# Rows through DRAM in place of PE's fan-out, constants in the order of need, and a new table of turns

## The chip, the cores and the metric

The kernel runs on one core of a Trainium2 chip. The metric is the device time of one execution in microseconds (us); the lower the better. All data are float32, except the adjacency matrix, which is int32.

## The reference

A batch of 32 graphs, each with 512 nodes of 256 features (`x`) and a 512 x 512 adjacency matrix (`adj`), goes through two layers. Both layers are a graph attention and a feed-forward part, each on the layer norm of `x` and added to `x`.

```
x += gat0(norm(x), adj)          # attention over neighbours, W and a
x += mamba2(norm(x))             # in-projection, causal conv of 4, scan over the
                                 # sequence in 8 heads of 64, 64 states, gate, out
x += gru(gat1(norm(x), adj), norm(x))
x += shared_mlp(norm(x)) + experts(norm(x))   # 4 experts, the best 2 weighted
```

Attention: `softmax(mask(leaky_relu(f1_i + f2_j, 0.2)))`, where f1 and f2 are products of a node's features with a vector. Since exp of a leaky relu is the larger of two products of a factor of the query and a factor of the key, the kernel needs two rows of 512 query factors on all 128 partitions. Mamba's scan needs, for chunks of 128 steps, the decay of the carried states for each head and step: exp of a cumulative sum, again a row on 64 partitions. The experts need the gate of each node on the 64 partitions that hold an expert's hidden units.

## The kernel before

The 32 elements of the batch are worked on one after the other and interleaved: each element passes through 20 parts (`PARTS`): `load_x`, `load_adj`, `gnn0`, `mamba`, `steps_of_time`, two convolutions, `products_of_bc`, `gate_of_z`, `scan`, `output`, `load_adj`, `gnn1`, two halves of the GRU, `gru_out`, `moe`, `gates`, `experts`, `mixture`. Every part is a generator that yields after each step, most steps being one instruction of one engine or a group of matmuls. `PLAN` gives each step a turn, and element b's steps come `PERIOD` turns after those of element b - 1. The steps of all elements, sorted by turn, are the program; each engine works through its share of it in that order and waits by semaphores for what it needs. In `PLAN` every turn modulo `PERIOD` is used once (420 steps, period 420), so a turn is a rank and not a time; one element's steps stretch over five periods.

Tiles rotate: `bank` (8 PSUM banks of 512 floats a partition), `big` (4), `quad` (16), `row` (26 of 512 floats). `x` and the adjacency rows are loaded, and the result stored, by DMAs that SP issues, in the same program order.

Three places put rows on many partitions with PE:

- `attention` (in both layers): `f1` of each 128 nodes is broadcast along the free dimension and transposed against `ident` (L290, four 128x128 transposes into `pf`), so that all partitions hold the 512 values. ACT makes the two factors of 128x512 from it (L294 relu, L297 exp, two each). `top`, `nf` and `nfs` (L276 to L285) are the maximum of the keys and its multiples. Then ACT and DVE build `pT` (L309 to L315), the weights of attention, for ps_h (layer 0, L343) or ps_g (layer 1, L675).
- `steps_of_time`: `byL` holds cumulative sums, 32 rows for each chunk c. After the ps_seg matmuls (L445) 24 matmul records with `kind1` (L461) put them on 64 partitions per head, into three banks `ps_ecs`, and ACT's exp makes `ecs` of three of the chunks (L468). `scan` uses them (L577, L579, L620).
- `gates`: the five columns of gates and a one are written four times over (`g5`, L797 to L807), transposed by four transposes (`ps_gT`, L812) and copied (`gT`, L815). `mixture` multiplies them with `pair_of` (L868) to put each expert's gate on 64 partitions, and adds the biases by matmuls on two row groups (L873); DVE multiplies (L877), PE sums the experts (L884, L886) and DVE adds to `x` (L888).

Float32 matmuls show as two records each, transposes as one.

Ahead of the loop come the constants: ACT issues most of their DMAs, SP those of layer 0's attention. PE multiplies weights there (`wc` L159, `wih` L174, `wrow` L125), and a pool `once` holds what only these need.

Of the kernel before, what the change touches and what calls it, by code (L numbers as in the profile page):

```python
# [11 lines left out]
F32 = mybir.dt.float32  # L12
# [6 lines left out]
P = 128  # L19
# [12 lines left out]
def adj_ffn_kernel(ctx: ExitStack, tc: tile.TileContext, i: dict, out: bass.AP):  # L32
# [5 lines left out]
    psum = ctx.enter_context(tc.tile_pool(name="psum", bufs=8, space=bass.MemoryType.PSUM))  # L38

# [4 lines left out]
    def big(name):  # L44
        return bigs.tile([P, T, N], F32, tag="big", name=name, bufs=4)
# [10 lines left out]
    stage = ExitStack()  # L56
    once = stage.enter_context(tc.tile_pool(name="once", bufs=1))
# [11 lines left out]
    pair_of = const.tile([HD, P], F32, name="pair_of")  # L69
    for j in range(2):  # L70
        nc.vector.tensor_copy(pair_of[32 * j:32 * j + 32].rearrange("e (s g) -> e s g", s=2),
                              ident[32 * j:32 * j + 32, 34 * j:34 * j + 2].unsqueeze(2).to_broadcast([32, 2, HD]))
# [8 lines left out]
    kind1 = const.tile([P, HD], F32, name="kind1")  # L81
    nc.vector.tensor_copy(kind1, kinds[:, 1:].to_broadcast([P, HD]))
# [3 lines left out]
    def load(name, shape, src, pool=const):  # L86
        t_ = pool.tile(shape, F32, name=name)
        nc.scalar.dma_start(t_, src)
        return t_
# [4 lines left out]
    def gat_columns(l, w, queue):  # L94

        ab = once.tile([P, 2 * D], F32, name="ab", tag="ab")
        queue.dma_start(ab, i[f"L{l}_gnn_a"].partition_broadcast(P))
        prod = once.tile([P, D], F32, name="prod", tag="prod")
        cols = once.tile([P, 2, KD], F32, name="cols", tag="cols")
        for k in range(KD):  # L100
            for s in range(2):
                nc.vector.scalar_tensor_tensor(prod, w[:, k, :D], 1.0, ab[:, s * D:(s + 1) * D], op0=ALU.mult,
                                               op1=ALU.mult, accum_out=cols[:, 1 - s, k:k + 1])
        return cols


# [4 lines left out]
    w_last = once.tile([P, D], F32, name="w_last")  # L111
    nc.sync.dma_start(w_last, i["L0_gnn_W"][D - 1].partition_broadcast(P))
    for k in range(KD):
        nc.vector.tensor_sub(we[:, k, :D], we[:, k, :D], w_last)
    nc.gpsimd.memset(we[:, 0, D:], 0.0)
    nc.vector.tensor_copy(we[:, 1, D:], ident[:, P - 1:])

    def on_all(l, w, queue):

        cols = gat_columns(l, w, queue)  # L120
        row_ = const.tile([P, 2, D], F32, name=f"wrow{l}")
        ps = bank("ps_wrow")
        for u in range(2):
            for k in range(KD):
                nc.tensor.transpose(ps[:, u * D + k * P:u * D + (k + 1) * P],  # L125
                                    cols[:, u, k:k + 1].to_broadcast([P, P]), ident)
        nc.vector.tensor_copy(row_.rearrange("p u d -> p (u d)"), ps)
        return row_

    wrow0 = on_all(0, we, nc.sync)  # L130
    scales = const.tile([P, 3], F32, name="scales")
    for n, v in enumerate((0.2, 0.8, -0.8)):
        nc.gpsimd.memset(scales[:, n:n + 1], v)


    win = load("win", [P, KD, 1160], kchunks(i["L0_ffn_W_in"]))
    nc.gpsimd.tensor_scalar(win[:, :, :512], win[:, :, :512], 0.5, 1.0, op0=ALU.mult, op1=ALU.mult)
    wdt = const.tile([P, KD, 32], F32, name="wdt")
    nc.gpsimd.memset(wdt, 0.0)
    nc.vector.tensor_copy(wdt[:, :, :HEADS], win[:, :, 1152:])  # L140
    cw = load("cw", [P, 5, 4], i["conv_w"])
    nc.vector.tensor_scalar_mul(cw, cw, 0.5)
    cb = load("cb", [P, 5], i["conv_b"])
    nc.vector.tensor_scalar_mul(cb, cb, 0.5)
    dtb = load("dtb", [P, HEADS], i["L0_ffn_dt_bias"].partition_broadcast(P))
    posneg = const.tile([P, 2, HEADS], F32, name="posneg")
    nc.scalar.dma_start(posneg[:, 0, :], i["L0_ffn_A_log"].partition_broadcast(P))
    nc.scalar.activation(posneg[:, 0, :], posneg[:, 0, :], AF.Exp)
    nc.vector.tensor_scalar_mul(posneg[:, 1, :], posneg[:, 0, :], -1.0)
# [3 lines left out]
    woutT = load("woutT", [P, KD, 512], kchunks(i["woutT"]), once)  # L153
    wlin = load("wlin", [P, KD, D], kchunks(i["L0_ffn_W_lin"]), once)
    wc = const.tile([P, NP, D], F32, name="wc")
    for j in range(NP):
        ps = bank("ps_wc")
        for k in range(KD):
            nc.tensor.matmul(ps[:, :D], woutT[:, k, j * P:(j + 1) * P], wlin[:, k, :], start=k == 0,  # L159
                             stop=k == KD - 1)  # L160
        nc.vector.tensor_scalar_mul(wc[:, j, :], ps[:, :D], normw[:, j:j + 1])


    w = load("w", [P, KD, D], kchunks(i["L1_gnn_W"]), once)
    wrow1 = on_all(1, w, nc.scalar)
    wT = load("wT", [P, KD, D], kchunks(i["L1_gnn_WT"]), once)
    raw = load("raw", [P, KD, 3 * D], kchunks(i["wihT"]), once)
    wih = const.tile([P, KD, 3 * D], F32, name="wih")
    for m in range(KD):
        for cols in (slice(0, 2 * D), slice(2 * D, 3 * D)):  # L170
            ps = bank("ps_wih")
            n = cols.stop - cols.start
            for k in range(KD):
                nc.tensor.matmul(ps[:, :n], wT[:, k, m * P:(m + 1) * P], raw[:, k, cols], start=k == 0,  # L174
                                 stop=k == KD - 1)
            nc.vector.tensor_copy(wih[:, m, cols], ps[:, :n])
# [3 lines left out]
    brz = const.tile([P, 4], F32, name="brz")  # L180
    nc.vector.tensor_add(brz, bih[:, :4], bhh[:, :4])
    nc.vector.tensor_scalar_mul(brz, brz, 0.5)

# [6 lines left out]
    for e in range(4):  # L190
        nc.scalar.dma_start(ew1[:, :, e, :], kchunks(i["L1_ffn_eW1"][e]))
# [6 lines left out]
    for r in (64, 96):  # L198
        nc.scalar.dma_start(b3[r:r + 4, :], i["L1_ffn_eb3"])
        nc.scalar.dma_start(b3[r + 4:r + 5, :], i["L1_ffn_sb3"].unsqueeze(0))  # L200
    gw = const.tile([P, KD, 32], F32, name="gw")
    nc.gpsimd.memset(gw, 0.0)
    nc.scalar.dma_start(gw[:, :, :4], kchunks(i["L1_ffn_gW"]))
    gb = load("gb", [P, 4], i["L1_ffn_gb"].partition_broadcast(P))

# [5 lines left out]

    stage.close()
    bigs = ctx.enter_context(tc.tile_pool(name="bigs", bufs=1))
    work = ctx.enter_context(tc.tile_pool(name="work", bufs=1))
    small = ctx.enter_context(tc.tile_pool(name="small", bufs=2))
# [41 lines left out]
    def load_x(e):  # L257
        e.x = quad("x", T)
        nc.sync.dma_start(e.x, x_in[e.b].rearrange("(t p) d -> p t d", p=P))
        yield  # L260

    def load_adj(e):

        e.adj = []
        for j in range(T):
            a_ = row("adj", I32)
            nc.sync.dma_start(a_, adjT_in[e.b, j * P:(j + 1) * P, :])
            e.adj.append(a_)
            yield

    def attention(f1, f2, adj, kind):

        top = small.tile([P, 1], F32, name="top")
# [8 lines left out]
        nfs = small.tile([P, 3], F32, name="nfs")  # L284
        nc.vector.tensor_scalar_mul(nfs, scales, nf)  # L285
# [3 lines left out]
        for t in range(T):  # L289
            nc.tensor.transpose(pf[:, t * P:(t + 1) * P], f1[:, t:t + 1].to_broadcast([P, P]), ident)  # L290
        yield
        query = quad("query", 2)
        for n, scale in enumerate((-0.8, 0.8)):
            nc.scalar.activation(query[:, n, :], pf, AF.Relu, scale=scale, bias=nfs[:, n + 1:n + 2])  # L294
            yield
        for n in range(2):
            nc.scalar.activation(query[:, n, :], query[:, n, :], AF.Exp, scale=-1.0)  # L297
            yield
# [7 lines left out]
        for j in range(0, T, 2):  # L306
            both = [(i, pT[:, i, :]) for i in (j, j + 1)]
            for i, p in both:
                nc.scalar.activation(p, query[:, 0, :], AF.Identity, scale=key1[:, i:i + 1])  # L309
                yield  # L310
            for i, p in both:
                nc.vector.scalar_tensor_tensor(p, query[:, 1, :], key2[:, i:i + 1], p, op0=ALU.mult, op1=ALU.max)  # L312
                yield
            for i, p in both:
                nc.vector.scalar_tensor_tensor(p, adj[i].bitcast(kind), 2.0 ** -120, p, op0=ALU.max, op1=ALU.min)  # L315
                yield
        return pT

    def scores(xn, wrow):

        f21 = small.tile([P, 2, T], F32, name="f21")
        for u in range(2):
            for t in range(T):
# [3 lines left out]
                yield  # L327
        return f21

    def gnn0(e):  # L330
# [4 lines left out]
        f21 = yield from scores(xn, wrow0)  # L335

        pT = yield from attention(f21[:, 1, :], f21[:, 0, :], e.adj, U32)
# [28 lines left out]
    def narrow(name, w, vT):  # L366
# [8 lines left out]
        few = small.tile([P, P], F32, name="fewT")  # L375
# [6 lines left out]
    def steps_of_time(e):  # L382
# [51 lines left out]
        yield  # L434
        byHL = quad("byHL", HEADS)
# [5 lines left out]
        e.ecss = [None]  # L441
        for h0 in (0, 4):
# [5 lines left out]
            for c in range(0, T, 2):  # L448
# [4 lines left out]
                for L, _ in both:  # L453
                    nc.scalar.activation(L, L, AF.Exp, scale=-1.0)
                    yield

        banks = [bank("ps_ecs") for c in range(1, T)]
        for q in range(2):
            for c, ps in enumerate(banks, 1):
# [435 lines left out]
    class Element:  # L895
        def __init__(self, b):
            self.b = b
# [97 lines left out]
```

## Time and profile before

| | |
|---|---|
| median of 3 runs | 3431.39 us (3430.87 to 3433.0) |
| profiled execution: its own time | 3430.99 us |
| its span, from the first to the last instruction | 3429.3 us |
| granted clock of TensorE, mean | 0.996 |
| PE / DVE / ACT / POOL busy | 3367.4 / 2814.7 / 1694.0 / 587.8 us |
| DMA: packets, MB | 78392, 110.45 |
| first ps_h (L343) | at 38.0 us |
| landing of adj (256 KB) / x (512 KB) / the result (512 KB), median | 2.8 / 3.9 / 5.3 us |

PE is TensorE's matmuls, PEld its weight loads, DVE VectorE, ACT ScalarE, POOL GpSimd, SP SyncE. A busy time is the time during which at least one instruction of the engine runs; matmuls are pipelined and overlap, so what one costs is better read from the distance between the starts of neighbours. "Idle before" names what an engine waited for. L with a number is a line of the kernel above.

### The profile page before, as it was taken

The page shows a single profiled execution, that of the slowest core. Times are in us where ns is not written, and L with a number is a line of the kernel's source. Part 1 is how long each engine was busy: PE and PEld are TensorE (multiplying, and loading weights), DVE is VectorE, ACT ScalarE, POOL GpSimd, SP SyncE. Part 2 cuts the span into 40 slices and gives each one's busy share as a digit, 9 for nine tenths or more (in the row PEclk, how much of TensorE's full clock was granted, in tenths as well). Part 3 has the DMA queues.
Part 4 walks back from the last instruction along what each step waited for, and adds up shares of the span by engine and source line. Part 5 has one row for each costly group of instructions (what it writes and reads, how often), then busy time and mean ns, then how long its engine had stood idle before and what let it go on. Part 6 is the DMA issues. An engine that isn't in the chain of part 4 may idle for free.

```text
span 3429.3 us, 49262 instructions
## 1 busy us (share of the span) xinstructions
PE 3367.4 (98%) x17800; PEld 1979.2 (58%) x17800; DVE 2814.7 (82%) x7625; ACT 1694.0 (49%) x3202; POOL 587.8 (17%) x593
## 2 busy tenths in 40 slices
PE   5999999999999999999999999999999999999998
PEld 3555655565555656555655556565556555565654
DVE  6888888888888888888888888888888888888873
ACT  2455455444555454554445554445544455544453
POOL 0112111112111121111121111221111211112210
PEclk8999999999999999999999999999999999999999
DMA  3001011011001010110110110101101100101000
GB/s 127 22 28 38 22 38 28 25 38 38 23 28 34 29 38 22 37 28 25 38 38 22 28 34 29 38 22 38 28 26 38 38 22 28 35 28 38 19 19 13
DMA packets 78392, 110.45 MB, mean 32 GB/s; under 512 B 8122, under 2 KB 44100, under 8 KB 78148
## 3 DMA queue, kind: packets, MB, share of 16 engines
q1 hardware_dynamic: 71216, 101.34, 9.9%
q10 hardware_dynamic: 6932, 5.96, 0.5%
q8 instruction: 141, 2.31, 0.3%
q14 instruction: 103, 0.84, 0.1%
HBM read 90.50 MB, written 16.78 MB: 31 GB/s over the span
## 4 chain that ended last, share of the span: by engine, by line
PE 95%; DVE 2%; issue 1%; ACT 0%; POOL 0%; DMA 0%; SPq 0%; DVEq 0%; POOLq 0%; ACTq 0%
PE ps_conv L476 8%; PE ps_g L675 7%; PE ps_rz L701 6%; PE ps_mo L657 6%; PE ps_e L837 6%; PE ps_z L538 6%; PE ps_h L343 6%; PE ps_rz L704 6%; PE ps_y L612 3%; PE ps_s L828 3%; PE ps_e L886 3%; PE ps_hn L714 3%; PE ps_g L351 3%; PE ps_in L726 3%; PE ps_seg L445 3%; PE ps_xT L252 2%
## 5 line engine op out<-in xcount | busy, mean ns | idle before, releaser
L483 DVE SCALAR_TENSOR_TENSOR acc<-ps_conv,cw,acc 128x511 f32<-128x511 f32 (+2 forms) x480 | 345.3, 736 | 51.0 <-ACT acc L480 46.5
L734 POOL TENSOR_TENSOR oT<-xT,gate 128x512 f32<-128x512 f32 x64 | 121.0, 1912 | 1130.0 <-ACT gate L731 1130.0
L476 PE MATMUL ps_conv<-xT,win 128*128 128x512 f32 x640 | 291.4, 594 | 0.2 <-ACT xT L254 0.2
L224 POOL TENSOR_TENSOR rstd<-rstd,mhalf 128x4 f32<-128x4 f32 x128 | 160.7, 1256 | 737.9 <-DVE dtd L556 380.4
L254 ACT COPY xT<-ps_xT 128x512 f32<-128x512 f32 x192 | 106.1, 587 | 300.5 <-PE ps_xT L252 300.5
L675 PE MATMUL ps_g<-xn,pT 128*128 128x257 f32 x1024 | 246.9, 383 | 0.7 <-DVE pT L315 0.7
L675 PEld LDWEIGHTS ps_g<-xn,pT 128*128 128x128 f32 x1024 | 191.6, 190 | 92.9 <-issue 37.5
L701 PE MATMUL ps_rz<-xT,whh 128*128 128x512 f32 x512 | 244.0, 599 | 1.2
L538 PE MATMUL ps_z<-xT,win 128*128 128x512 f32 x512 | 242.0, 595 | 0.0
L704 PE MATMUL ps_rz<-go,wih 128*128 128x512 f32 x512 | 240.7, 592 | 0.0
L343 PE MATMUL ps_h<-pT,xn 128*128 128x512 f32 x512 | 231.8, 596 | 8.8 <-issue 8.8
L837 PE MATMUL ps_e<-xT,ew 128*128 128x512 f32 x512 | 236.6, 595 | 0.0
L579 POOL TENSOR_TENSOR ecs<-ecs,cc 128x512 f32<-128x512 f32 x96 | 136.1, 1418 | 546.3 <-DVE end L577 538.0
L657 PE MATMUL ps_mo<-wc,xh 128*128 128x256 f32 x1024 | 226.3, 379 | 0.0
L312 DVE SCALAR_TENSOR_TENSOR pT<-query,key,pT 128x512 f32<-128x512 f32 x256 | 212.0, 859 | 9.9 <-ACT pT L309 9.9
L657 PEld LDWEIGHTS ps_mo<-wc,xh 128*128 128x128 f32 x1024 | 192.1, 190 | 24.8
L476 PEld LDWEIGHTS ps_conv<-xT,win 128*128 128x128 f32 x640 | 121.7, 190 | 140.3 <-issue 137.1
L234 DVE BATCH_NORM_STATS2 st<-x 128x6 f32<-128x256 f32 x512 | 196.6, 416 | 3.3
L480 ACT ACTIVATE acc<-ps_conv,cb,cw 128x512 f32<-128x512 f32 x160 | 124.8, 780 | 138.0 <-PE ps_conv L476 137.4
L241 DVE TENSOR_SCALAR xn<-x,mv,rstd 128x256 f32<-128x256 f32 (+1 forms) x512 | 183.3, 410 | 5.4 <-POOL rstd L224 5.4
L325 DVE SCALAR_TENSOR_TENSOR prod<-xn,wrow 128x256 f32<-128x256 f32 x512 | 187.6, 417 | 0.0
L682 ACT ACTIVATE pT<-ps_g,rs 128x256 f32<-128x256 f32 x128 | 60.7, 474 | 236.8 <-DVE rs L679 236.8
(209 smaller groups left out, 7040.3 us busy)
## 6 DMA issues: line engine op xcount, KB each, us to landing
adj<-in_adjT_dram SPq DMA_DIRECT2D x256, 256.0 KB, 2.8
x<-in_x_dram SPq DMA_DIRECT2D x32, 512.0 KB, 3.9
out_dram<-x SPq DMA_DIRECT2D x32, 512.0 KB, 5.3
win<-in_L_ffn_W_in_dram ACTq DMA_DIRECT2D x1, 1160.0 KB
raw<-in_wihT_dram ACTq DMA_DIRECT2D x1, 768.0 KB, 7.4
whh<-in_whhT_dram ACTq DMA_DIRECT2D x1, 768.0 KB, 8.1
ew<-in_L_ffn_eW_dram ACTq DMA_DIRECT2D x5, 128.0 KB, 3.1
woutT<-in_woutT_dram ACTq DMA_DIRECT2D x1, 512.0 KB, 7.5
```

The source lines that it names most:

```text
L234: nc.vector.bn_stats(st[:, t, :], x[:, t, :])
L312: nc.vector.scalar_tensor_tensor(p, query[:, 1, :], key2[:, i:i + 1], p, op0=ALU.mult, op1=ALU.max)
L325: nc.vector.scalar_tensor_tensor(prod, xn[:, t, :D], 1.0, wrow[:, u, :], op0=ALU.mult, op1=ALU.mult, accum_out=f21[:, u, t:t + 1])
L343: nc.tensor.matmul(ps, xn[:, j, k * P:(k + 1) * P], pT[:, j, :], start=j == 0, stop=j == T - 1)
L476: nc.tensor.matmul(ps, win[:, k, 512 + c * P:512 + (c + 1) * P], e.xT[:, k, :], start=k == 0, stop=k == KD - 1)
L483: nc.vector.scalar_tensor_tensor(acc[:, s:], ps[:, :N - s], cw[:, c, 3 - s:4 - s], acc[:, s:], op0=ALU.mult, op1=ALU.add)
L538: nc.tensor.matmul(ps, win[:, k, j * P:(j + 1) * P], uT[:, k, :], start=k == 0, stop=k == KD - 1)
L657: nc.tensor.matmul(ps[:, :D], xh[:, j, t * P:(t + 1) * P], wc[:, j, :], start=j == 0, stop=j == NP - 1)
L675: nc.tensor.matmul(ps[:, :D + 1], pT[:, j, cut], xn[:, j, :], start=j == 0, stop=j == T - 1)
L701: nc.tensor.matmul(ps, whh[:, k, cols], xT[:, k, :], start=k == 0, stop=False)
L704: nc.tensor.matmul(ps, wih[:, k, cols], e.go[:, k, :], start=False, stop=k == KD - 1)
L837: nc.tensor.matmul(ps, ew1[:, k, m, :], vT[:, k, :], start=k == 0, stop=k == KD - 1)
```

## The change

1. **Query factors.** One transpose instead of four puts f1 of the 512 nodes, twice over, into eight rows of 128 (`f21` gets a third row, a copy). ACT makes both factors in one relu and one exp of 8x128, with a scale that differs by partition (`slopes`). SP writes the eight rows of 512 bytes to a line in DRAM and reads it back onto all 128 partitions as `query`.
2. **Decays of states.** ACT takes exp of `byL` (128x128), SP writes it to DRAM (`rows`), and twelve DMAs (three chunks, four each) read rows of 512 bytes onto 64 partitions. The matmuls L461 and their exp are gone. The reads are a part of their own, `decays_of_states`.
3. **Gates.** `g5` is written once, transposed once; the copy goes to DRAM (`gates`), and four DMAs read each expert's four rows of 512 bytes onto 64 partitions (`pg`). L868 is gone; the bias matmuls use four row groups, the outputs four banks with 256 columns each.
4. **Constants.** All their loads are issued by SP, in the order of first need, those of element 0's `x` and adjacency among them. The products of weights move into `prepare_gnn0`, `prepare_mamba`, `prepare_output`, called just ahead of element 0's part of that name. Raw weights lie in tiles of the loop (`row`, `quad`, `big`) instead of the pool `once`.
5. **Table.** 428 steps, period 428, all turns new.

The diff, cut to its core:

```diff
+    dram = ctx.enter_context(tc.tile_pool(name="dram", bufs=3, space=bass.MemoryType.DRAM))
...
     def load(name, shape, src, pool=const):
-        nc.scalar.dma_start(t_, src)
+        nc.sync.dma_start(t_, src)
...
+    first = Element(0)
+    for _ in load_x(first):
+        pass
...
+    def prepare_output():
+        for j in range(NP):
+            ps = bank("ps_wc")
...
+        on_all(1, w1)
...
+                nc.scalar.copy(wih[:, m, cols], ps[:, :n])
...
         pf = bank("ps_f1")
-        for t in range(T):
-            nc.tensor.transpose(pf[:, t * P:(t + 1) * P], f1[:, t:t + 1].to_broadcast([P, P]), ident)
+        nc.tensor.transpose(pf[:2 * T, :P], f21[:, 1:, :].rearrange("p u t -> p (u t)"), ident)
+        yield
+        q8 = small.tile([P, P], F32, name="fewT", bufs=4)[:2 * T, :]
+        nc.scalar.activation(q8, pf[:2 * T, :P], AF.Relu, scale=slopes[:2 * T, 1:2], bias=nfs[:2 * T, 1:2])
+        yield
+        nc.scalar.activation(q8, q8, AF.Exp, scale=-1.0)
+        yield
+        line = dram.tile([2 * T, P], F32, name="line")
+        nc.sync.dma_start(line, q8)
         yield
         query = quad("query", 2)
-        for n, scale in enumerate((-0.8, 0.8)):
-            nc.scalar.activation(query[:, n, :], pf, AF.Relu, scale=scale, bias=nfs[:, n + 1:n + 2])
-            yield
-        for n in range(2):
-            nc.scalar.activation(query[:, n, :], query[:, n, :], AF.Exp, scale=-1.0)
-            yield
+        nc.sync.dma_start(query.rearrange("p n (t m) -> p (n t) m", t=T), line.partition_broadcast(P))
+        yield
...
+        nc.vector.tensor_copy(f21[:, 2, :], f21[:, 1, :])
+        yield
...
+        eE = small.tile([P, P], F32, name="fewT", bufs=4)
+        nc.scalar.activation(eE, byL, AF.Exp)
+        yield
+        e.rows = dram.tile([P, P], F32, name="rows")
+        nc.sync.dma_start(e.rows, eE)
...
-        banks = [bank("ps_ecs") for c in range(1, T)]
-        for q in range(2):
-            for c, ps in enumerate(banks, 1):
+    def decays_of_states(e):
+        for c in range(1, T):
+            ecs = row("ecs").rearrange("p (j l) -> p j l", j=NP)
+            for q in range(2):
                 for r in range(2):
-                    nc.tensor.matmul(ps[r * HD:(r + 1) * HD, q * 2 * P:(q + 1) * 2 * P], kind1[32 * c:32 * c + 32, :],
...
+                    src = e.rows[32 * c + HEADS + h.start:32 * c + HEADS + h.stop:2, :]
+                    nc.sync.dma_start(ecs[r * HD:(r + 1) * HD, 2 * q:2 * q + 2, :], src.partition_broadcast(HD))
...
-        for t in range(T):
-            nc.tensor.transpose(ps[:, t * P:(t + 1) * P], g5[:, t, :, :].rearrange("p r e -> p (r e)"), ident)
+        nc.tensor.transpose(ps[:, :P], g5.rearrange("p t e -> p (t e)"), ident)
...
+        line = dram.tile([P, P], F32, name="gates")
+        nc.sync.dma_start(line, gT)
...
+        for j in range(2):
+            pg = row("pg")
+            for s in range(2):
+                src = line.rearrange("(t e) p -> e t p", t=T)[2 * j + s]
+                nc.sync.dma_start(pg[s * HD:(s + 1) * HD, :].rearrange("g (t p) -> g t p", t=T),
+                                  src.partition_broadcast(HD))
...
-        for j, pg in enumerate(pgs):
-            own = slice(32 * j, 32 * j + 32)
-            nc.tensor.matmul(pg, pair_of[own, :], gT[own, :], start=True, stop=True)
...
+        pes = [bank("ps_e3") for t in range(T)]
+        for t, ps in enumerate(pes):
+            own = slice(32 * t, 32 * t + 32)
+            nc.tensor.matmul(ps[:, :D], gT[own, :], b3[own, :], start=True, stop=False)
...
-    PERIOD = 420
+    PERIOD = 428
...
+                if b == 0 and PARTS[n] in prepare:
+                    prepare[PARTS[n]]()
```

Turns of the new table that the prediction speaks of. Layer 1: top's transpose 878, pf 881, relu and exp 882 and 883, line 886, adj2 889, adj3 902, x of the element two later 907 (its own turn 51), fan-out 910, first pT on ACT 914, last pT on DVE 928, first ps_g 931. Layer 0: pf 153, exp 159, line 160, fan-out 161, first pT 194, first ps_h 249. Decays: rows 628, reads 630, 637, 722, their uses in the scan 702, 740, 763. Gates: copy 1572, line 1624, reads 1630 and 1662, products 1681 and 1683.

## The prediction

> **What bounds the kernel now.** I read the page's busy times first, then the stretches of time, the waits of PE, the groups by shape, and the timeline around the groups that the change touches. From the page:
>
> ```profile
> span 3429.3 us, 49262 instructions
> ...
> PE 3367.4 (98%) x17800; PEld 1979.2 (58%) x17800; DVE 2814.7 (82%) x7625; ACT 1694.0 (49%) x3202; POOL 587.8 (17%) x593
> ...
> PE 95%; DVE 2%; issue 1%; ACT 0%; POOL 0%; DMA 0%; SPq 0%; DVEq 0%; POOLq 0%; ACTq 0%
> ```
>
> A stretch from the middle (columns: stretch, its length, then busy time with count of PE, PEld, DVE, ACT and POOL, the granted clock, DMA share, GB/s):
>
> ```profile
> 1000.00:2000.00 1000.00, 998.36 (x5364) 590.35 (x5364) 839.06 (x2258) 499.48 (x946) 181.06 (x177) 1.00 0.11 31
> ```
>
> PE is the bound: 95% of the chain that ends last, and idle 1.6 us in 1000 here. It works in program order, and the table of turns keeps it fed. Nearly all of its 62 us of idle time lies at the edges: by the same view 38.6 us in the first 100 us, 6.9 in the next 100, some 12 in the last 130. So what PE no longer does in the middle comes off the time, unless PE then waits. PE's waits for DVE's pT, the step that the change delays, come to 0.7 us in the whole run.
>
> How much it no longer does is read from starts, not from busy time (columns: start, length, instruction, count):
>
> ```profile
> 1511.23 0.60 PE L290 MATMUL ps_f<-ident,f 128*128 128x128 f32 x4
> 1511.67 1.88 PE L704 MATMUL ps_rz<-go,wih 128*128 128x512 f32 x4
> ...
> 1519.63 0.70 PE L868 MATMUL ps_gb<-gT,pair_of 32*128 32x512 f32 x2
> ...
> 1520.82 1.99 PE L701 MATMUL ps_rz<-xT,whh 128*128 128x512 f32 x4
> ...
> 1543.64 1.11 PE L461 MATMUL ps_ecs<-byHL,kind 32*64 32x256 f32 x24
> 1544.68 0.66 PE L586 MATMUL ps_st<-xdd,bt 128*64 128x128 f32 x8
> ...
> 1601.03 0.60 PE L812 MATMUL ps_gT<-ident,g 128*128 128x128 f32 x4
> 1601.46 1.88 PE L538 MATMUL ps_z<-xT,win 128*128 128x512 f32 x4
> ```
>
> From one start to the next: four transposes 0.44 and 0.43 us, the gates' fan-out with the bias matmuls (they overlap) 1.19, the decays' 24 records 1.04, four records of 128x512 1.72 (0.43 each).
>
> **What the Trainium skill says.** "Perfetto Trace Analysis", section Identifying the Most-Contended Engine: matmul busy time misleads because matmuls are pipelined. Agreed: one 128x512 record lasts 0.59 us and costs 0.43. "TensorE: Matmul & The Clock Gate", section Measured speedup vs the span model: four row tiles (K=32, N=512) run 3.07 times as fast as one after another. Agreed: eight ps_seg records of that shape take 1.07 us between starts (89.94 to 91.01) where eight times 0.43 is 3.44. "DMA: Bandwidth & Descriptors", section Latency and other measured facts: the receipt of the written bytes dominates a fixed cost of some 2 us, and HBM is the slowest target. The direction agrees: a load of 512 KB lands after 3.9 us, a store of 512 KB after 5.3. The same page, section Queues, rings and completion order: descriptors of one queue are taken in ring order on each DMA engine. No view here isolates that; I use it for one rival.
>
> **Part by part, per element (32 of them).**
> - Query factors, twice: four transposes become one. Three times 0.11, twice: 0.65 us off PE.
> - Decays of states: 24 records go, 1.04 us.
> - Gates: three of four transposes go, 0.32. Fan-out: only eight bias records of 32x256 stay, now on four row groups; 8 x 0.215 / 3 = 0.57 us against 1.19, so 0.62 off. Bounds: 0.43 (perfect overlap) to 1.0 (little of it).
> - Sum 2.63 us, **84 us** over 32. If a lone transpose between big matmuls shows 0.27 us instead of 0.11 (its own length, L290's mean) and the bias matmuls overlap badly, 1.8 us, 58 in all.
> - ACT: four activations of 128x512 per attention go (0.684 and 0.627, 5.2 us per element), three ecs (0.597) and half of the gT copy; five small ones come (0.28 each, from the 128x128 copy of L376). Some 6 us less; ACT was at 49%, so that itself buys nothing.
> - DVE: two copies of 4 columns (0.15 each), four adds of 128x256 (0.414, L594's shape) for two of 0.68, one small product for four of 0.166: +0.1 us. The products with the gates take 0.674 from PSUM and, by L636, 0.683 from SBUF. DVE stays at 88 us per element, now of 102.6: 86%. Cover: PE's own 102.6 us.
> - POOL: one memset of 0.46 becomes about 0.2; covered, POOL is at 17%.
> - SP: per element 10 DMAs become 32: a line and a fan-out twice, rows and twelve for the decays, a line and four for the gates. At 0.33 to 0.43 us of issue (the adj and x rows) 13 us of 102: no bound. Packets: 4608 of 512 B per element. From x (32 packets of 1 KB per DMA engine, 3.9 us) and adj (8 of 2 KB, 2.8 us) a KB costs about 0.06 us on one engine, a landing 1.7 us besides; all the new ones cost 4608/16 x 0.03 to 0.076 us (the latter the mean of all packets in the page) = 9 to 22 us of 102, beside a DMA share of 0.11. No bound either; their latency is.
> - Every step of every part gets a new turn. I lay the table out in PE work, with 0.43 per 128x512 record and so on. It sums to 101.5 us per element (the old one by the same prices to 104.2; the trace has 105).
>
> **The new waits.** SP, in order, waits for exp, writes the line, waits for its landing, then reads it back 128 times; behind it on SP stand the next adj loads, needed 19 us of PE work later. ACT's first pT waits for the fan-out, and queued behind it on ACT are other elements' evictions, on DVE everything behind the pT steps, on PE all that follows ps_g or ps_h. No gain is possible here: PE has nothing to win but 1.6 us in 1000. Layer 0: from pf to the first ps_h lie 16.5 us of PE work: room. **Layer 1 is the tight place**: between top's transpose and the first ps_g lie one output group of the mixture (1.29), eight groups of 1.72 and two transposes: 15.3 us. Into that must fit nf and nfs (1.0, as in the trace: 1588.4 to 1589.4), relu and exp (0.5), line and fan-out, and pT up to its last DVE step (6.4: from ACT's 1591.99 to DVE's 1598.35). That leaves 7.4 us for both DMAs. Estimate: the line 1.7 to 3.1 (1.4 more for a store, as out against x), the fan-out 1.7 + 64 packets x 0.03 to 0.045 (half as much again, if part of the price is per packet) = 3.6 to 4.6; together 5.3 to 7.7. But in SP's order adj2, adj3 and x, 1 MB, stand between the two and can be 0 to 2 us ahead of the fan-out in the rings. I take 0.5 us of PE idle per element: **+16 us**; bounds 0 and 4.3 (rival 2). The decays' rows have 17 us or more, except chunk 3's (8 us for four loads of 64 KB); the gates' have 4.7 us from the last load to its use, against about 3 (adj's 2.8): nothing. Nor for buffers: by the table at most 13 of the 26 rows are held at once, and the mixture needs four banks as before.
>
> **The edges.** Before, PE did the weight products (wc 5.2, wrow 0.7, wih 5.3 us) while it waited for element 0 anyway; they now stand at the first output, in a stretch where PE had 6.9 us of idle time in 100. I charge 10. All constants, 48 DMAs, now go through SP ahead of element 0's line. Before, ACT was through with its own at 32.5 and ps_h came at 38.0; the bytes are nearly the same (8 MB at 220 to 320 GB/s), so SP is through at 30 to 35, line and fan-out take 6, pT 3.5: ps_h at 42 to 45. That is 4 to 7. Together **+16** (5 to 28: the products may fill gaps, or SP may be slower alone). At the end the last attention has less foreign PE work to hide 6 us of DMA under: **+5** (0 to 10); the gates' fan-out there lies under some 9 us of expert matmuls.
>
> **Sum.** The profiled run took 3431.0 (span 3429.3 and 1.7 around it), the median is 3431.4: no difference. 3431 - 84 + 16 + 16 + 5 = **3384 us**.
>
> **Rivals.**
> 1. Everything is covered, the products fill idle time: 3431 - 84 + 5 = 3352. For: chains as tight as the new one leave PE 0.16% idle now (before, 10.9 us of PE work from pf to ps_g for some 10 us of chain). Against: two landings per attention that no view here has measured.
> 2. **Slower: the fan-out of layer 1 comes late.** It takes PE's idle time one for one, 32 times. The gain less the edges is 63 us, so from 63 / 32 = 2.0 us of lateness the change loses. With the line at 3.1, the fan-out at 4.6 and 2 us of x and adj ahead of it: 9.7 of 7.4 allowed, 2.3 late, 74 us: 3442; at 76 ns per packet (6.6 for the fan-out) 4.3 late, 3506. For: SP's order and the ring. Against: the middle of my estimate for the two, 6.5, fits in the 7.4, and x and adj load while the line is still landing.
> 3. The change doesn't remove what it says: lone transposes and bias matmuls at the poor prices. 3431 - 58 + 16 + 16 + 5 = 3410.
>
> **Chances.** My forecast (3362 to 3400) 0.50; rival 1 0.17; rival 3 (3400 to 3424) 0.13; rival 2 0.20, of which 0.13 is slower and the rest no change or a small loss. 0.2%, 7 us, is about what a measurement of this kernel can tell from no change. So faster 0.80, same 0.07, slower 0.13. The range reaches from rival 1's 3346 to 3440, leaving out most of rival 2's slower half.
>
> **What would show it.** Right: PE busy near 3285, the four groups above gone or cut to a quarter, DVE near 2820, ACT near 1510. The new waits: ACT's pT on a DMA; PE's ps_g on DVE's pT, near 16 us in all. ps_h of element 0 at 42 to 45. Wrong: ps_g waiting over 60 us (rival 2), PE idle in the middle from another chain (dtd, the gates' products), the bias group near 1.0 us (rival 3), or PE busy down by less than 60.

## The result and the profile after

The kernel after takes 3424.23 us (median of 15 runs, 3420.84 to 3431.31) beside 3431.95 us (15 runs of the kernel before on the same chip). The ratio is 0.998, with an interval of 0.9973 to 0.9987. It is faster, by 7.7 us or 0.2%; the forecast was 47. The number lies inside the outer range (3346 to 3440), but outside the 3362 to 3400 of the forecast proper: most of the expected gain is missing.

The profiled execution of after took 3430.65 us, 6 above its median, so the two traces, which differ by only 0.4 us, show where time moved rather than the gain. From the page of after: the busy times and the shares of the chain that ended last.

```profile
PE 3281.2 (96%) x16616; PEld 1920.2 (56%) x16616; DVE 2917.6 (85%) x7650; ACT 1527.9 (45%) x3016; POOL 543.4 (16%) x591
...
PE 76%; DVE 11%; issue 6%; DMA 4%; ACT 2%; SPq 1%; POOL 0%; DVEq 0%; ACTq 0%; POOLq 0%
```

PE's work went as forecast: 86 us less busy, where 84 were expected. The time did not follow, because PE's idle time rose from 62 to 148 us: its share of the chain fell from 95% to 76%. DVE, which was to gain 5 us of work, gained 103. The same stretch from the middle, with the columns of the one shown for before:

```profile
1000.00:2000.00 1000.00, 983.46 (x5084) 577.58 (x5083) 885.71 (x2319) 461.85 (x916) 168.27 (x178) 1.00 0.18 55
```

PE is now idle 16.5 us in 1000, where it was 1.6.

POOL's add of `blin` to `x` happens once per element and so marks a period. Cut at the third and at the last of these adds, the two profiled executions read as follows (differences in us; the forecast's terms are spread over the same stretches):

| stretch | before | after | PE busy | PE idle | sum | forecast |
|---|---|---|---|---|---|---|
| up to the third add | 216.8 | 247.1 | -2 | +32 | +30 | with the tail |
| 29 periods | 3034.6 | 2977.4 | -100 | +43 | -57 | -76 + 14.5 = -62 |
| after the last add | 177.9 | 204.4 | +16 | +10.5 | +26.5 | edges together +15 |

The last column's 15 is the 21 charged for the edges, less 2.13 for each of three elements. So the middle came out near the forecast, through two errors of opposite sign, and the edges failed: of the 46 us between the forecast and the change of the profiled execution, 42 lie there.

**Why PE wins 3.45 us per element and not 2.63.** The timeline of before, PE at ps_seg (start, length, instruction, count):

```profile
1528.21 2.12 PE L445 MATMUL ps_seg<-byHL,byS 32*128 32x512 f32 x8
1530.26 0.70 PE L884 MATMUL ps_e<-sw,h 128*128 128x256 f32 x2
```

and of after:

```profile
1540.85 2.00 PE L464 MATMUL ps_seg<-byHL,byS 32*128 32x512 f32 x16
1542.78 1.55 PE L356 MATMUL ps_h<-pT,xn 128*128 128x512 f32 x3
```

Before, eight records took 2.05 us here; after, sixteen take 1.93. The same matmuls were busy for 102.5 us in all before and for 65.8 after. The time lost before lies inside the records, counts as busy, and is in no list of waits. That it was a wait for PSUM banks is an inference from what follows when banks are held longer (`b2_gates_alone` below).

**Where PE now waits.** The waits of PE in after (engine, group, line, releaser: total us, times, longest):

```profile
PE ps_o L764 <- DVE oT L755: 32.6, 31, 2.2
PE ps_h L356 <- DVE pT L326: 23.3, 1, 23.3
...
PE ps_g L692 <- DVE pT L326: 12.2, 18, 2.0
...
PE ps_o L764 <- DVE fewT L823: 9.8, 29, 0.4
```

Three separate things stand here. In each element PE waits 1.3 us at ps_o, the transposes of the GRU's output (the first and the last of these lines together; fewT holds the gates, which DVE makes between the GRU's last steps): a place that the prediction never looked at. The single 23.3 us is element 0's first attention. Layer 1's ps_g, which was to wait 16 us, waits 12.2.

**ps_o: DVE comes late, and POOL holds it up.** Three groups of DVE in before (busy us, mean ns, then idle before):

```profile
L877 DVE TENSOR_TENSOR e<-e,ps_gb 128x512 f32<-128x512 f32 x64 | 40.7, 674 | 5.2 <-PE ps_gb L868 5.2
L436 DVE TENSOR_TENSOR byHL<-byL,head 128x1024 f32<-128x1024 f32 x32 | 39.2, 1225 | 1.1
L494 DVE SCALAR_TENSOR_TENSOR xh<-xh,acc 128x512 f32<-128x512 f32 x128 | 115.9, 906 | 2.5
```

and in after:

```profile
L890 DVE TENSOR_TENSOR e<-e,pg 128x512 f32<-128x512 f32 x64 | 104.8, 1638 | 14.5 <-ACT e L849 14.5
L456 DVE TENSOR_TENSOR byHL<-byL,head 128x1024 f32<-128x1024 f32 x32 | 65.7, 2055 | 1.1
L511 DVE SCALAR_TENSOR_TENSOR xh<-xh,acc 128x512 f32<-128x512 f32 x128 | 87.5, 684 | 0.0
```

`byHL` is the same instruction on the same data and takes 0.83 us longer, 26 us in all. The product with the gates was to cost the same from SBUF as from PSUM and takes 0.96 longer, 64 us in all. But `xh`, a product of the convolutions, takes 28 us less. So DVE's 103 us are a net sum, in which the layer norm's `xn` (L262, 32 us more) and `sq` (L661, 30 us less) also count. The timeline of after shows what runs beside `byHL` and the gates' product:

```profile
1742.22 3.48 POOL L751 TENSOR_TENSOR oT<-xT,gate 128x512 f32<-128x512 f32 x2 [16.64 <-ACT gate L748]
...
1742.41 2.17 DVE L456 TENSOR_TENSOR byHL<-byL,head 128x1024 f32<-128x1024 f32 x1
1744.50 2.42 DVE L323 SCALAR_TENSOR_TENSOR pT<-query,key,pT 128x512 f32<-128x512 f32 x2
...
1753.38 0.69 DVE L755 SCALAR_TENSOR_TENSOR oT<-oT,gate 128x512 f32<-128x512 f32 x1
...
1752.81 0.30 PE L764 MATMUL ps_o<-ident,oT 128*128 128x128 f32 x1 [0.32 <-DVE fewT L823]
1754.13 0.98 PE L764 MATMUL ps_o<-ident,oT 128*128 128x128 f32 x7 [1.02 <-DVE oT L755]
...
1788.52 2.35 POOL L376 TENSOR_TENSOR x<-x,blin 128x1024 f32<-128x1024 f32 x1
1788.63 2.80 DVE L890 TENSOR_TENSOR e<-e,pg 128x512 f32<-128x512 f32 x1
...
1791.95 0.68 DVE L890 TENSOR_TENSOR e<-e,pg 128x512 f32<-128x512 f32 x1
```

While POOL subtracts the GRU's n from x (L751), `byHL` takes 2.17 us, not 1.22, and a pair of pT steps 2.42, not 1.40: 2 us later for all that stands behind them on DVE. The GRU's last steps (L755) stand there, and PE waits for them. While POOL adds `blin`, the gates' product takes 2.80 us; half a microsecond after the end of both, the next takes 0.68.

The Trainium skill, "SBUF — State Buffer", says in the section Who interferes with whom that a VectorE instruction with two SBUF inputs contends with a GpSimd instruction that reads SBUF, and in the section Summary: rules for kernel authors that the second of the two to issue blocks fully. The trace agrees: blocked until POOL's end at 1790.87 and then running for 0.68, the product would take 2.92. `byHL`, held until the first of the two subtractions is through (1.27 us, the shortest of L751 in the trace), would take 2.30. It also fits that the product with a PSUM operand took 674 ns before.

The collision of the product with `blin` is new. That of POOL's subtraction is not. The same place in before:

```profile
1730.69 1.22 DVE L436 TENSOR_TENSOR byHL<-byL,head 128x1024 f32<-128x1024 f32 x1
1732.00 1.60 DVE L494 SCALAR_TENSOR_TENSOR xh<-xh,acc 128x512 f32<-128x512 f32 x1
1733.52 1.76 DVE L312 SCALAR_TENSOR_TENSOR pT<-query,key,pT 128x512 f32<-128x512 f32 x1
...
1740.37 0.69 DVE L738 SCALAR_TENSOR_TENSOR oT<-oT,gate 128x512 f32<-128x512 f32 x1
...
1730.91 3.82 POOL L734 TENSOR_TENSOR oT<-xT,gate 128x512 f32<-128x512 f32 x2 [35.16 <-ACT gate L731]
...
1741.21 1.07 PE L747 MATMUL ps_o<-ident,oT 128*128 128x128 f32 x8
```

Here `byHL` starts 0.22 us ahead of POOL and runs undisturbed. `xh` and pT, behind it, pay instead: 1.60 and 1.76 us, where 0.68 and 0.74 are usual, again 2 us. So it matters which of the two starts first. In three elements of after `byHL` is ahead of POOL too, by 0.03 to 0.10 us, and takes 1.22 or 1.23; then the pair of pT steps pays it all (3.45 us in one of them).

What changed is the room. From the start of `byHL` to the end of the last oT DVE takes 11.7 us in after (1742.41 to 1754.07) and 10.4 in before (1730.69 to 1741.06): eight pT steps of layer 0 stand between in the new order, three in the old, with `xh`, `g` and `e`. PE comes to ps_o 10.1 us after the start of `byHL` in after (1752.49, its 0.32 us of waiting taken off) and 10.5 in before. In before the last oT is ready 0.15 us ahead of ps_o; in after PE waits 1.3 us for it. These are readings of one element; the waits of the other middle elements are equal to it (0.32 to 0.36 and 1.02 to 1.03).

**Layer 1's fan-out.** The timeline of after, SP, ACT and PE:

```profile
1702.77 0.30 SPq L305 DMA_DIRECT2D line<-fewT  x1
1703.12 1.72 SPq L103 DMA_DIRECT2D adj<-in_adjT_dram  x2
1704.89 0.43 SPq L95 DMA_DIRECT2D x<-in_x_dram  x1
1705.65 0.33 SPq L308 DMA_DIRECT2D query<-line  x1
...
1711.97 1.34 ACT L320 ACTIVATE pT<-query,key 128x512 f32<-128x512 f32 x2 [4.03 <-DMA query<-line]
...
1716.25 2.38 PE L692 MATMUL ps_g<-xn,pT 128*128 128x257 f32 x8
```

The two DMAs take 9.2 us from SP's first issue to ACT's start, not the 5.3 to 7.7 estimated, and 6.3 of it is the fan-out alone. Over the run the two take 7.3 to 10.1 us in layer 1. In the middle PE waits at ps_g only in elements where they take 9.3 us or more (0.15 us at 9.31, 0.89 at 10.05). So the room is 9.2 us, not the prediction's 7.4. It is wider, as far as this timeline tells, because ps_g takes pT piece by piece: it starts at 1716.25, while DVE's last pT steps end at 1717.88. The lateness cost 0.4 us per element of idle and some 0.4 inside ps_g (busy 259.9 us, before 246.9).

**Element 0.** From the timeline of after:

```profile
33.63 0.29 SPq L305 DMA_DIRECT2D line<-fewT  x1
...
42.46 9.26 PE L356 MATMUL ps_h<-pT,xn 128*128 128x512 f32 x16 [23.27 <-DVE pT L326]
```

ACT had the factors ready at 20.46; SP stored them at 33.63, when it was through with all constants.

### The profile page after: what moved, and what is told of

Its sections match the earlier page's. It is cut to its first block, busy times and chain, and to the rows that moved or that the text cites. A ratio compares the mean times of both kernels' runs of the same rounds, so it can differ in the third digit from the quotient of the medians.

```text
span 3428.9 us, 48462 instructions
## 1 busy us (share of the span) xinstructions
PE 3281.2 (96%) x16616; PEld 1920.2 (56%) x16616; DVE 2917.6 (85%) x7650; ACT 1527.9 (45%) x3016; POOL 543.4 (16%) x591
## 4 chain that ended last, share of the span: by engine, by line
PE 76%; DVE 11%; issue 6%; DMA 4%; ACT 2%; SPq 1%; POOL 0%; DVEq 0%; ACTq 0%; POOLq 0%
PE ps_g L692 7%; PE ps_e L864 6%; PE ps_conv L493 6%; PE ps_mo L674 6%; PE ps_z L555 5%; PE ps_rz L721 4%; DMA query<-line 4%; PE ps_rz L718 3%; PE ps_y L629 3%; PE ps_h L356 3%; PE ps_in L743 3%; DVE pT L323 3%; PE ps_g L364 3%; PE ps_e L902 3%; PE ps_xT L273 2%
## 5 line engine op out<-in xcount | busy, mean ns | idle before, releaser
L245 POOL TENSOR_TENSOR rstd<-rstd,mhalf 128x4 f32<-128x4 f32 x128 | 129.4, 1011 | 1194.8 <-DVE rstd L243 1038.9
L323 DVE SCALAR_TENSOR_TENSOR pT<-query,key,pT 128x512 f32<-128x512 f32 x256 | 213.9, 876 | 107.9 <-ACT pT L320 107.9
L493 PE MATMUL ps_conv<-xT,win 128*128 128x512 f32 x640 | 300.9, 601 | 0.0
L692 PE MATMUL ps_g<-xn,pT 128*128 128x257 f32 x1024 | 259.9, 392 | 12.4 <-DVE pT L326 12.2
L356 PE MATMUL ps_h<-pT,xn 128*128 128x512 f32 x512 | 237.0, 607 | 23.3 <-DVE pT L326 23.3
L320 ACT ACTIVATE pT<-query,key 128x512 f32<-128x512 f32 x256 | 172.3, 710 | 148.0 <-DMA query<-line 148.0
L718 PE MATMUL ps_rz<-xT,whh 128*128 128x512 f32 x512 | 235.4, 592 | 0.0
L262 DVE TENSOR_SCALAR xn<-x,mv,rstd 128x256 f32<-128x256 f32 (+1 forms) x512 | 215.3, 474 | 6.0 <-POOL rstd L245 5.9
L255 DVE BATCH_NORM_STATS2 st<-x 128x6 f32<-128x256 f32 x512 | 206.2, 420 | 6.6
L849 ACT ACTIVATE e<-ps_e,eb 128x512 f32<-128x512 f32 x192 | 127.6, 680 | 176.7 <-PE ps_e L864 174.7
L751 POOL TENSOR_TENSOR oT<-xT,gate 128x512 f32<-128x512 f32 x64 | 112.4, 1778 | 581.7 <-ACT gate L748 581.7
L657 ACT ACTIVATE sq<-xh 128x512 f32<-128x512 f32 x128 | 79.9, 631 | 255.1 <-DVE xh L653 253.7
```

The costliest lines, as they stand in the source:

```text
L255: nc.vector.bn_stats(st[:, t, :], x[:, t, :])
L262: nc.vector.tensor_scalar(xn[:, t, :width], x[:, t, :width], mv[:, t, 0:1], r[:, t:t + 1], op0=ALU.subtract, op1=ALU.mult)
L356: nc.tensor.matmul(ps, xn[:, j, k * P:(k + 1) * P], pT[:, j, :], start=j == 0, stop=j == T - 1)
L493: nc.tensor.matmul(ps, win[:, k, 512 + c * P:512 + (c + 1) * P], e.xT[:, k, :], start=k == 0, stop=k == KD - 1)
L692: nc.tensor.matmul(ps[:, :D + 1], pT[:, j, cut], xn[:, j, :], start=j == 0, stop=j == T - 1)
L718: nc.tensor.matmul(ps, whh[:, k, cols], xT[:, k, :], start=k == 0, stop=False)
```

## Experiments

Ratios are to the kernel before on the same chip (medians 3431.38 to 3433.12 us), as are the differences of the parts run alone. All other differences are between the median of a kernel and that of after (3424.23); single runs of after spread over 10 us, so 2 or 3 us mean nothing here.

**POOL's subtraction left out** (`e3_no_subtraction`), and in a second kernel **moved to DVE** (`e3b_subtraction_on_dve`). The first kernel has only the removed line of this diff, the second both.

```diff
-        nc.gpsimd.tensor_sub(q, xT[:, m, :], n)
+        nc.vector.tensor_sub(q, xT[:, m, :], n)
```

> The changed kernel without POOL's subtraction in the GRU (x - n, two steps of 128x512 per element are left out, q keeps its old value). Theory (DVE is slowed while POOL runs a two-operand step of its own): byHL falls from 2.06 to about 1.22 us, the pT step beside it from 1.8 to 0.75, PE's waits of ps_o for DVE from 42 us to under 12, the time by 25 to 40 us, to about 3390. Rival (the loss in the middle is the latency of the new DMAs, or the GRU's chain is long for another reason): DVE's durations stay, ps_o waits as before, the time changes by less than 6 us.

> The changed kernel with the GRU's subtraction on DVE instead of POOL; the result is the reference's. Theory (collision of DVE and POOL): byHL and pT go back to 1.22 and 0.75 us, DVE loses two steps of 0.68 for it, some 0.6 us per element are left over, and ps_o waits 0.7 us per element instead of 1.3: the time falls by 12 to 25 us from the changed kernel's 3424. Rival (leaving the subtraction out had shortened the GRU's chain, and that was its gain): ps_o waits as long as in the changed kernel or longer, the time is the same or up to 25 us longer.

Without it: 3374.87 us, ratio 0.9828 (0.9812 to 0.9845), 49 less than after. `byHL` is back at 1225 ns, and PE's wait at ps_o for oT has fallen from 32.6 us to 2.1, the last element's. The middle stretch of this kernel:

```profile
1000.00:2000.00 1000.00, 997.67 (x5144) 589.84 (x5144) 881.32 (x2347) 469.07 (x927) 133.88 (x160) 1.00 0.19 57
```

PE is as full as before the change. On DVE, where the step stays, the time is 3403.92 us, ratio 0.9922 (0.9907 to 0.9936), 20 less than after; the pages have DVE at 2894 us there, at 2854 without the step and at 2918 in after, so the step takes 40 us on DVE and saves it 63. PE's wait at ps_o for oT is 27.2 us there, and the 9.8 us on fewT are gone.

The runs show that in the new order the collision costs at least 20 us. The other 29 are then either the subtraction's place in the chain or its 40 us on DVE. No run parts the two, but the trace of after speaks for the second. POOL's result lies ready at 1745.70, and DVE comes to use it at 1751.27 (L753). Over all 64 of these steps DVE's idle time before L753 is 2.1 us, and none of it ended on POOL:

```profile
L753 DVE SCALAR_TENSOR_TENSOR oT<-gate,oT 128x512 f32<-128x512 f32 x64 | 43.5, 679 | 2.1 <-ACT gate L724 2.1
```

It fits that DVE takes 9.7 us from the start of `byHL` to the last oT without the step and 11.0 with the step its own, where after has 11.7. The pT steps (L323) had a mean of 859 ns before, 876 after, and 746 with the step on DVE. No run takes the subtraction out of the old order; there PE hardly waits at ps_o (3.7 us in the whole run, in two waits), though the 2 us of delay are there.

**POOL's add of blin left out** (`e6_no_blin`).

```diff
-        nc.gpsimd.tensor_add(e.x, e.x, blin.unsqueeze(1).to_broadcast([P, T, D]))
```

> The kernel after without POOL's add of blin to x (L376), which this kernel leaves out. Theory (a collision with POOL costs time only where PE waits next for DVE): e*pg (L890) falls from 1638 to about 690 ns, DVE's busy time by some 60 us to about 2857, but PE's wait at ps_o on oT stays near 33 us and the time falls by less than 6 us: 3418 to 3426. Rival (DVE's busy time as such is what costs, 85% being too near to full): the time falls by a good part of the 60 us, to 3375 to 3400.

3425.70 us (14 runs), ratio 0.998 (0.9972 to 0.9988): no difference from after that these runs can tell. The group of the product:

```profile
L889 DVE TENSOR_TENSOR e<-e,pg 128x512 f32<-128x512 f32 x64 | 43.7, 684 | 14.5 <-ACT e L848 14.5
```

PE's wait at ps_o for oT is 32.6 us, as in after.

One collision, 61 us of DVE's busy time, costs nothing to be seen; the other, some 60 (26 on `byHL`, 33 on pT), costs at least 20. What differs is whether PE waits next for what is queued behind it.

**The fan-out ahead of the adjacency rows in SP's order** (`e2_fanout_first`: turns of the table; fan-out 889, adj2 902, adj3 910).

```diff
-        (736, 781, 889, 902),
+        (736, 781, 902, 910),
...
-         869, 870, 871, 872, 873, 874, 878, 879, 880, 881, 882, 883, 886, 910, 911, 914, 915, 919, 920, 921,
+         869, 870, 871, 872, 873, 874, 878, 879, 880, 881, 882, 883, 886, 889, 911, 914, 915, 919, 920, 921,
```

> The changed kernel with three turns of layer 1 exchanged, so that SP issues the fan-out right behind the line and ahead of adj2, adj3 and x. Theory (1 MB ahead in the rings delays the fan-out): it is issued some 1.3 us after the line instead of 2.9 and lands after some 4.3 us instead of 6.2; ACT's waits for the fan-out fall from 129 us (without element 0's) to under 60, ps_g's wait for pT from 12 us to under 4, the time by 8 to 25 us. Rival (the fan-out itself takes 6 us, or what is left is DVE's lateness at ps_o): ACT waits as before, or it waits less and ps_o takes over what ps_g gives back; less than 5 us.

3406.96 us, ratio 0.9928 (0.9913 to 0.9943), 17 less than after. ACT's wait for the fan-out, 148.0 us in after, in this kernel:

```profile
ACT pT L320 <- DMA query<-line: 55.3, 33, 19.4
```

PE's wait at ps_g falls from 12.2 to 2.5 us, and ps_o stands unchanged at 32.6. Line and fan-out now mostly take 5.2 to 6.6 us in layer 1. A period takes 102.15 us where after has 102.67: 15 us over 29, of the 26 by which these two profiled executions differ.

**Constants behind element 0's fan-out** (`e1_late_constants`: all from `win` on are collected in a list, as the first below, and issued at turn 161 of element 0).

```diff
-    win = load("win", [P, KD, 1160], kchunks(i["L0_ffn_W_in"]))
+    win = load_later("win", [P, KD, 1160], kchunks(i["L0_ffn_W_in"]))
...
+            if (b, n, PLAN[n][k]) == (0, 2, 161):
+                for t_, src in waiting:
+                    nc.sync.dma_start(t_, src)
```

> The changed kernel, with the DMAs of all constants from win on issued on SP after element 0's first fan-out instead of before its line; nothing else moves. Theory (order on SP): the line leaves at about 20.6 us instead of 33.6, the first ps_h starts at 30 instead of 42.5, and the time falls by 10 to 13 us, to about 3412. Rival (the bytes bound the start, or win comes too late for the first convolution): the first ps_h is earlier but a later wait takes its place; less than 4 us.

3408.97 us, ratio 0.9929 (0.9914 to 0.9944), 15 less. PE's wait at its first ps_h is 9.7 us, 13.6 shorter, and the third blin add comes at 232.6 instead of 247.1 us.

**Each part alone in the table of before.** The three parts with rows through DRAM, one at a time, with the table and constants of before.

> The kernel before with its own table, and of the change only the decays of states through DRAM: exp, rows and the twelve reads are issued at the turn of byHL, the turns of the 24 matmuls and their exps stay empty; 25 rows instead of 26 and four buffers of fewT. Theory (what PE no longer does comes off the time if the table is kept): 1.04 us per element, 33 us, about 3398, PE idle still near 62 us. Rival (SP's new waits hold up the adj loads, or the DMAs slow other engines): PE waits in ps_h or ps_g for pT, gain under 15 us.

The decays alone (L461's matmuls and exp out; rows and twelve reads issued behind the exp of `byL`): 3404.66 us, ratio 0.9919 (0.9904 to 0.9934). That is 28 us, of the 33 expected; PE is busy 40 less, of which 14 are ps_seg's (88.5 us; the three banks of `ps_ecs` are free). With the order of before, PE now waits where the kernel after waits, and where before hardly did:

```profile
PE ps_o L750 <- DVE oT L741: 21.7, 31, 2.6
```

A ps_seg group ahead of this place takes 1.57 us here, not 2.05, so PE comes 0.5 us earlier, and the old order had almost nothing to spare. `byHL` and POOL stand as in before.

> The table and all else of the kernel before; only the query factors go through DRAM (line, fan-out), issued where ACT's exp stood. Theory (the chain does not fit in the old table): in layer 1 10.9 us of PE work lie between pf and the first ps_g there, and the chain is nf and nfs 1.0 + relu and exp 0.5 + line 1.3 + fan-out 4.5 + pT 6.4 = 13.7, of which some 1 can lie under ps_g itself; so PE waits 1.5 to 2.5 us at ps_g in each element and wins 0.65 us from the six transposes: time 3455 to 3490, PE's wait at ps_g on pT 50 to 80 us. Rival (the pieces of the chain overlap enough, the new table was not needed for this part): ps_g waits under 15 us in all, time 3405 to 3420.

The query factors alone (diff as in part 1 of the change, turns of the old activations): 3547.15 us, ratio 1.0338 (1.0321 to 1.0355), 115 slower. The direction was right, the size not: 3455 to 3490 was expected. PE's waits:

```profile
PE ps_g L684 <- DVE pT L322: 42.4, 37, 3.2
PE ps_gT L821 <- DVE g L816: 39.0, 30, 1.3
```

The theory counted only ps_g. PE waits for the gates `g` (L816) as well, 1.3 us in each element; on DVE they stand behind the late pT steps. And PE's busy time rose by 31 us although it has 192 records less (ps_z and ps_g are 41 us longer inside their records). The old table has too little room for this chain.

> The kernel before with its own table, and of the change only the gates through DRAM (one transpose, line and four reads at the turn of the copy, bias matmuls on four row groups, four output banks); 25 rows. Theory: 0.32 for the transposes and 0.5 to 0.6 for the fan-out per element, 26 to 30 us, about 3403. Rival (the products with the gates, now from SBUF, run beside POOL and delay the output, or the reads hold up SP): PE waits in ps_e or at the next x, gain under 12 us.

> The kernel before with the gates through DRAM as in b2_gates_alone, but the bias matmuls two and two just ahead of their outputs, so that at no time more banks are held than in the kernel before. Theory (b2 lost because four banks were held from the bias matmuls on, and ps_seg waited for banks inside its matmuls): ps_seg back from 4.6 to 3.2 us of busy time per element or less, the time 3405 to 3415. Rival (the loss came from the gates' DMAs or from SP's order): ps_seg improves little, the time stays above 3460.

The gates alone: 3490.01 us, ratio 1.0169 (1.0154 to 1.0184), 57 slower, which neither theory had. ps_seg's busy time rose from 102.5 to 148.2 us: the bias matmuls take four banks at once and hold them until the experts are done, and ps_seg finds none. With the bias matmuls two and two, just ahead of their outputs,

```diff
-        for t, ps in enumerate(pes):
-            own = slice(32 * t, 32 * t + 32)
-            nc.tensor.matmul(ps[:, :D], gT[own, :], b3[own, :], start=True, stop=False)
...
+                if t % 2 == 0:
+                    for u in (t, t + 1):
+                        pes[u] = bank("ps_e3")
...
```

ps_seg falls to 74.0 us as expected, but the time only to 3457.97, ratio 1.0077 (1.0060 to 1.0094), still 27 slower. In place of it PE now waits at

```profile
PE ps_o L749 <- ACT L L453: 54.8, 29, 1.9
```

The releaser there, ACT's copy of ps_seg out of its banks (L453), fits a wait for a bank; no run shows it. So of the three parts only the decays gain in the old order: 28 us won against 115 and 57 lost (27 with the bias matmuls in pairs). Two of the three parts need another order; what the new table is worth without them was not run.

**The three repairs together** (`e5_three_together`: after with late constants, fan-out first, subtraction on DVE).

> The changed kernel with late constants, the fan-out ahead of adj2, adj3 and x, and the subtraction on DVE. If the three losses are apart from each other their gains add: 15 (measured for the first), 8 to 25 and 12 to 25 us, about 3375, below both kernels. If PE's waits only move from one place to the next (ps_g to ps_o), it is about 3395.

3371.28 us, ratio 0.9823 (0.9808 to 0.9838), faster than both kernels. Alone they gained 15, 17 and 20; together 53. In the middle stretch PE is busy 992.3 us of 1000.

## Why the prediction was right or wrong

- **PE's removed work: right in sum, for a partly wrong reason.** 84 us forecast, 86 measured over the run; in the 29 middle periods 3.45 us per element, not 2.63. The surplus of 0.8 is covered by ps_seg's hidden wait (36.7 us less over the run), which the trace of before could have shown: the prediction's 1.07 us for eight such records is one group of element 0, and in the middle of the same run a group of eight takes 2.05. At the edges PE is busy 14 us longer. By its records the tail holds 8 us more of PE work (808 of 519 per element, at 101.0 us, against 794 of 556 at 104.5); most of the rest goes with a lower granted clock there (0.94 in the last 129 us, before 0.98; 0.92 against 1.00 from 100 to 200 us). Why the clock was lower was not tried.
- **"DVE ... +0.1 us. ... Cover: PE's own 102.6 us": the step that failed in the middle.** The cover was argued from DVE's mean share, 86% of a period. PE waits for one step of DVE, not for its mean: ps_o waits for the GRU's last steps, and there the new order lacks 1.3 us in each element (42 us in all). POOL delays DVE by 2 us just ahead of them, in both orders; the old one hid it with nothing to spare, and the new one puts 1.3 us more of DVE's work in between and brings PE there 0.4 us earlier. Moving POOL's step off gives back 20 us, leaving it out 49. The price of +0.1 failed too, by 3.2 us per element: the product with the gates was priced from a row that ran undisturbed, and costs 64 us more beside POOL. That part cost no time.
- **Layer 1's fan-out, +16: nearly right, by two errors.** Line and fan-out took 7.3 to 10.1 us (5.3 to 7.7 forecast), and the rows of adj and x did stand ahead of them, as rival 2 feared. But the window was 9.2, not 7.4. Putting the fan-out first gave 17.
- **The store's price was too high.** In layer 0, where nothing stands between, the fan-out is issued 1.2 us after the line. The prediction took 1.7 to 3.1, and the Trainium skill, "DMA: Bandwidth & Descriptors" (section Latency and other measured facts), has some 2 us. For 4 KB the measurement decides. The packets were too many as well: 4608 more per element were forecast, and the pages have 109,588 more in the run, some 3400 per element.
- **The edges, +16 and +5: the term mis-sized most, and the one that makes up the missing gain.** ps_h of element 0 came at 42.46, inside the 42 to 45 forecast. But PE idled 32 us more up to the third element and 10.5 more after the last; with 14 us more of busy time the edges cost 57, where the table has 15 for them. Fifteen of the 57 are the constants ahead of the line, as `e1_late_constants` shows; `e2_fanout_first` takes off 8 at the start. The prediction set the delay of element 0 at 4 to 7 us and stopped there. It did not follow elements 0 and 1 further, where each step waits for one chain without foreign work beside it (ps_top 12.4 us, ps_E 4.5, ps_st 4.1 up to the third add). The rest, over 30 us with most of the tail, stays open: no run takes it apart.
- **The rivals.** Rival 1 (all covered) and rival 3 (little removed) are refuted by PE's idle and busy times. Rival 2's mechanism is there at a small part of its price (17 us). In the old order, in `b4_query_alone`, it is much of the loss (42 us at ps_g).

## What to carry to other kernels

An instruction's price holds only beside the neighbours it was measured with: a VectorE step with two SBUF operands that starts behind a GpSimd step took twice as long or more here. Whether this costs anything is decided by what PE waits for next, not by the sum: 61 us of such delay cost nothing to be seen, and some 60 cost at least 20. Nor is a delay that a trace shows always new. The 2 us behind POOL's subtraction were in the old order too, where nothing waited for them, so look for the room that was lost and not only for the step that is slow. An engine's mean share says nothing of this room. And a pipeline's edges have to be followed element by element: there every latency added to a chain shows, and constants that went ahead of the first chain on its queue cost 15 us.

## What the runs showed of the hardware

- VectorE's 128x512 product of two SBUF operands went from 0.68 to 2.80 us beside a GpSimd add of 2.35 us; without that add it takes 0.684 in the mean.
- Who starts first decides who pays: `byHL` took 1.22 us where it started 0.22 us ahead of GpSimd's subtraction (before), and 2.17 where it started 0.19 behind (after). Either way the VectorE steps there lost 2 us to the two subtractions.
- Waits inside matmul records count as PE busy: the same 512 ps_seg records took 65.8, 74.0, 102.5 or 148.2 us in four kernels. That the waits are for PSUM banks is inferred. PE's busy time and its list of waits can both miss such a wait.
- A line of 4 KB stored to DRAM could be read back after 1.2 us; its fan-out to 128 partitions, 512 KB in rows of 512 bytes, took 6.3 us behind a 512 KB and two 256 KB loads (5.7 to 8.3 over layer 1 of that run), and 3.9 to 5.0 in the middle elements with these loads put behind it (`e2_fanout_first`).
